# Three attention layers in one kernel: new due dates for the work between the attention steps, and rope computed in place

## The chip, the cores and the metric

One core of a Trainium2 chip runs the whole program. The core's engines work side by side, each with its own instruction queue: the tensor engine (PE in the profile; PEld is its weight load), the vector engine (DVE), the scalar engine (ACT), GpSimd (POOL) and the sync engine (SP), whose queue issues most of the transfers (DMA). The metric is the device time of one launch in microseconds. Lower is better.

## The reference, cut to what matters

The input `x` has 4 batches of 1024 tokens with 128 features. Four blocks follow one another, each of the form x + layernorm(block(layernorm(x))); all of it is float32. They are attention with 16 heads of 8 whose scores are clipped to [-10, 10]; a block with latent attention (heads of 64, half of which is rotated by position: rope) and a mixture of 8 experts; attention with 16 heads of 8 without the clip; and a low-rank feed-forward block with gelu.

```python
scores = jnp.clip(jnp.einsum('bhtd,bhsd->bhts', q, k) * SCALE, -10.0, 10.0) + mask   # first attention
q = jnp.concatenate([q_nope, _rope(q_rope)], axis=-1)                                # second
k = jnp.concatenate([kv, _rope(k_rope)], axis=-1)
x = x + _layernorm(_L0_attn_ref(_layernorm(x), ...))
x = x + _layernorm(_L0_ffn_ref(_layernorm(x), ...))
x = x + _layernorm(_L1_attn_ref(_layernorm(x), ...))
x = x + _layernorm(_L1_ffn_ref(_layernorm(x), ...))
```

## The kernel before

The program treats the work as three layers (classes `First`, `Second`, `Third`; the last feed-forward block is the tail of `Third`). A layer and a batch make a *stage*, twelve in all; a stage has four head groups `g` of four heads, and a stage and a head group make a *unit*: 48 units, numbered `n`, layer by layer and batch by batch. So units 0 to 15 are layer 1, 16 to 31 layer 2, and 32 to 47 layer 3.

**The main loop** (from line 1349) counts steps `at`, 20 to a unit. In each of ten iterations of a unit it issues the score products of one tile of keys (`scores`, the matmuls `ps_k<-strips`), the exponential on ACT with clip on DVE and causal cut on POOL (`weigh`, tile `pt`), and the products with the values of an earlier tile (`next_products`, the matmuls `av<-pt`). The argument of `next_products` says how many tiles may stay behind. Layers 2 and 3 subtract each row's maximum before the exponential. The maxima of a unit are made about one unit ahead, by `max_step` (matmuls `ps_q`, reductions on DVE into `mx`), at steps set by the queue `maxima`: 22 or 19 steps ahead of their unit. `negate` then sends the negated maxima by DMA into the unit's strips.

**Strips** are the tiles from which score products read queries and keys; there are three, unit `n` uses `n % 3`. `prepare(g, n)` of a layer fills them by DMA: from `packed` tiles in layers 1 and 3, from `rp` (rotated queries) and `lat` in layer 2, where the keys lie in a tile `kT` made by the preparation of the stage's first group. `roped` (line 661) does the rotation: ACT copies the product to `rb`, two DMAs write it with even and odd rows exchanged into `swapped`, DVE multiplies `rb` by the cosines into a new tile, and POOL multiplies `swapped` by the sines and adds it.

**All other work** is cut into pieces by Python generators (class `Task`). A piece says what it uses: LIGHT (vector, scalar, GpSimd or DMA work), SPARE or RING (a PSUM bank). There are intakes (`take_in`: normalise, transpose, project for a stage), preparations of units, tails of stages (`tail`: output projection, `add_normed`, experts), and `quarters` (the feed-forward of the last batch). After each iteration `other_work(at)` asks `pick` for pieces, up to four LIGHT ones and one of each other kind, and `pick` takes the task with the least slack: its due step, less the present step, less 1.35 for each piece that it has left. Nothing with a slack of 50 or more is taken, and unless it is late by 5, nothing while ACT or DVE are estimated to be behind PE. Due steps are 44 (layer 2), 28 (layer 3) or 8 (layer 1) ahead of the unit for a preparation, which can begin 48, 40 or 33 ahead; an intake is due 48, 40 or 33 ahead of its stage; a tail 5 steps before the end of the next stage.

**Forced work.** What is not done when it is needed is issued at once, in whole: `need_prep` before a unit and before its first maximum, `need_input`, `need_tail`, and `need_free(k)`, which runs a stage's tail until the result buffer that it reads (`att_free`) may be written again. It is called before the first result of a stage: with the stage before where either is of layer 2, otherwise with the stage before that, since the results lie in tiles of the tag `y` in `pool2` (`pool1` holds one of each tag, `pool2` two): a stage of layer 1 or 3 takes one, a stage of layer 2 both, one for each half of its tokens. A tail of layer 3 sets `att_free` when `add_normed` (line 427) has read the result in its first normalisation: statistics of 8 tiles on DVE (`stats`), the power -1/2 on POOL (`inv_root`), 8 scalings on ACT into `ynorm` (`scaled`), then two additions on POOL. In layers 1 and 2 it is set behind the first transposes.

PSUM's banks are given out in rotation: from layer 2 on a ring of 7 serves scores, maxima and most of the other work.

Of the kernel before, what the change touches and what calls it, by code (L numbers as in the profile page):

```python
# [138 lines left out]
def sandwich(ctx: ExitStack, tc: tile.TileContext, a: dict, out: bass.AP):  # L139
# [69 lines left out]
    w3_n = stage[:, 2048 : 2048 + 3 * D]  # L209
# [5 lines left out]
    later(out=w3_n, in_=a["L1_attn_w_qkv"])  # L215
# [66 lines left out]
    w3 = ctile([P, 3, D], "w3")  # L282
# [23 lines left out]
    def prepare_weights():  # L306
# [74 lines left out]
        nc.gpsimd.tensor_copy(w3.rearrange("p s e -> p (s e)"), w3_n)  # L381

# [87 lines left out]
    def project(packed, w, xT, copy):  # L470

        yield RING, 1
        t = pool2.tile([P, T], F32, tag=f"packed{len(packed)}", name="packed")
        packed.append(t)
        by_half(copy, t, product(w, xT, "ps_p"))
# [76 lines left out]
    class First:  # L552
# [43 lines left out]
        def take_in(self):  # L596
            self.xT = new_xT("xT1")
            self.unit = {}
            if self.b == 0:
                xn = pool1.tile([P, NT, D], F32, tag="xn", name="xn")  # L600
                self.packed = [pool2.tile([P, T], F32, tag=f"packed{s}", name="packed") for s in range(2)]
# [37 lines left out]
        def result(self, g, h):  # L639
            if g == 0 and h == 0:  # L640
                self.att = pool2.tile([P, NT, D], F32, tag="y", name="att1")
            return self.att[:, 4 * h : 4 * h + 4, 32 * g : 32 * g + 32]
# [18 lines left out]
    def roped(dst, w, xT):  # L661
# [6 lines left out]
        nc.vector.tensor_tensor(dst[0:n], rb[0:n], cos[0:n], ALU.mult)  # L668
        for c in range(2):
            yield LIGHT, 2 * (1 - c)  # L670
            cols = slice(512 * c, 512 * c + 512)
            nc.gpsimd.tensor_tensor(swapped[0:n, cols], swapped[0:n, cols], sin[0:n, cols], ALU.mult)  # L672
            nc.gpsimd.tensor_tensor(dst[0:n, cols], dst[0:n, cols], swapped[0:n, cols], ALU.add)

    class Second:
# [41 lines left out]
        def prepare(self, g, n):  # L717
            if g == 0:
# [3 lines left out]
                self.kT = pool2.tile([P, T], F32, tag="packed0", name="kT2")  # L722
# [3 lines left out]
                rp = pool2.tile([P, T], F32, tag="packed1", name="rpk")  # L726
                yield from roped(rp, wkr.rearrange("p j r -> p (j r)"), self.xT)
                yield LIGHT, 2
                for j in range(2):
                    nc.sync.dma_start(out=self.kT[64 * j + 32 : 64 * j + 64], in_=rp[32 * j : 32 * j + 32])  # L730
            if g % 2 == 0:
# [4 lines left out]
                by_half(nc.scalar.copy, lat, product(w, self.xT, "ps_l"))  # L736
            yield RING, 1
            rp = pool2.tile([P, T], F32, tag="packed1", name="rp")
            yield from roped(rp, w2r[:, 4 * g : 4 * g + 4].rearrange("p h r -> p (h r)"), self.xT)
            yield LIGHT, 2  # L740
            while step_now[0] < strips_free(n):
                yield LIGHT, 1
            t = self.unit[g] = strips[n % 3]
            nc.sync.dma_start(
                out=t[R:P:64].rearrange("o s (q c) -> o (s q) c", q=NT),
                in_=no_max[0:2].unsqueeze(1).to_broadcast([2, 2 * NT, P]),
            )
            for j in range(4):
                pp, at, h = j // 2, 64 * (j % 2), 4 * (g % 2) + j
                nc.sync.dma_start(out=t[at : at + R, pp, :], in_=self.lat[R * h : R * h + R, :])  # L750
                nc.sync.dma_start(out=t[at + 32 : at + 64, pp, :], in_=rp[32 * j : 32 * j + 32, :])
# [197 lines left out]
    class Third:  # L949
# [8 lines left out]
        def take_in(self):  # L958
            self.unit = {}
            self.xT = new_xT("xT3")  # L960
# [7 lines left out]
        def prepare(self, g, n):  # L968
            yield LIGHT
            if n < 2 * B * NG + 3:  # L970
                clear(strips[n % 3])
# [23 lines left out]
        def result(self, g, h):  # L995
            if g == 0 and h == 0:
                self.y = pool2.tile([P, NT, D], F32, tag="y", name="y3")
# [47 lines left out]
        def quarter(self, num, k):  # L1045
# [11 lines left out]
            if k == 1:  # L1057
                work, xb = tile("rb"), pool2.tile([P, T], F32, tag="packed0", name="xb")
# [70 lines left out]
    def ahead(u):  # L1129

        return (48, 44) if u.width == R else (40, 28) if u.has_max else (33, 8)
# [3 lines left out]
    units = [(layer[b], g) for layer in layers for b in range(B) for g in range(NG)]  # L1135
    stages = [u for layer in layers for u in layer]
    inputs = [Task(u.take_in(), u.pieces[0]) for u in stages]
    prep = [Task(u.prepare(g, n), (9, 4, 5, 4)[g] if u.width == R else 1) for n, (u, g) in enumerate(units)]
    tails = [None] * len(stages)
# [3 lines left out]

    def need_tail(k):

        while tails[k] is None or not tails[k].done:
            behind.popleft()[1].finish()

    def need_free(k):

        while not stages[k].att_free:
            behind[0][1].look(step_now[0])
            behind[0][1].piece(step_now[0])
            if behind[0][1].done:
                behind.popleft()

    def need_prep(n):
        for i in range(n + 1):
            if not prep[i].done:
                need_input(i // NG)  # L1160
                prep[i].finish()

    def need_input(k):
        for i in range(k + 1):
# [4 lines left out]

    def max_tiles(n):  # L1170

        mx, beside = {}, units[n][0].width != R
        for h in range(2):
            tiles = max_parts_of(h)
            if h and not beside:
                tiles = [tiles[i] for i in (0, 4, 1, 5, 2, 6, 3)]
            for i, parts in enumerate(tiles):
                for pp in (1, 0) if beside else (0, 1):
                    yield n, h, parts, pp, mx, i == len(tiles) - 1 and pp == 1 - beside

    def max_step(n, h, parts, pp, mx, last):
# [4 lines left out]
        ps = rtile("ps_q")  # L1186
        for qt, c, at, w in parts:
            for jj in range(2):
                q, k = u.rows(g, pp, jj)
                nc.tensor.matmul(  # L1190
# [239 lines left out]
```

## Time and profile before

| | |
|---|---|
| Runs | 2199.86, 2203.24, 2202.6 us: median 2202.6 |
| Profiled execution | 2196.13 us, of which the profile's span is 2194.4 |
| PE busy | 2062.8 us (94%), mean granted clock 0.974 |
| DVE, ACT, POOL busy | 1457.2 (66%), 1251.0 (57%), 589.5 (27%) us |
| Data moved by DMA | 42.93 MB in 32245 packets |
| Units 16, 32 and 47 begin | about 512.8, 1445.4 and 2109.4 us |

Busy time of an engine is time in which one of its instructions runs. The granted clock is the share of full speed that PE was allowed. A step is 1/20 of a unit, so that step 300 is the middle of unit 15, step 320 the start of layer 2, and step 640 that of layer 3.

### The profile page before, as it was taken

The page shows a single profiled execution, that of the slowest core. Times are in us where ns is not written, and L with a number is a line of the kernel's source. Part 1 is how long each engine was busy: PE and PEld are TensorE (multiplying, and loading weights), DVE is VectorE, ACT ScalarE, POOL GpSimd, SP SyncE. Part 2 cuts the span into 40 slices and gives each one's busy share as a digit, 9 for nine tenths or more (in the row PEclk, how much of TensorE's full clock was granted, in tenths as well). Part 3 has the DMA queues.
Part 4 walks back from the last instruction along what each step waited for, and adds up shares of the span by engine and source line. Part 5 has one row for each costly group of instructions (what it writes and reads, how often), then busy time and mean ns, then how long its engine had stood idle before and what let it go on. Part 6 is the DMA issues. An engine that isn't in the chain of part 4 may idle for free.

```text
span 2194.4 us, 40088 instructions
## 1 busy us (share of the span) xinstructions
PE 2062.8 (94%) x14480; PEld 939.4 (43%) x14480; DVE 1457.2 (66%) x4201; ACT 1251.0 (57%) x2360; POOL 589.5 (27%) x840
## 2 busy tenths in 40 slices
PE   7999999789999999999999999899999999999994
PEld 3334333334444544454444444344444444444432
DVE  4677776477666675567556675368778678777755
ACT  4777778524554554355534544255556766766775
POOL 3343333223232211222122311121113233323332
PEclk9999999989999999999999999899999999999996
DMA  2310000011111100111011100000000000000000
GB/s 59 69 17 11 12 11 11 21 38 25 28 42 26 25 16 22 35 29 26 6 30 35 29 13 1 11 7 7 6 7 7 12 7 16 8 11 17 7 1 20
DMA packets 32245, 42.93 MB, mean 20 GB/s; under 512 B 11552, under 2 KB 23840, under 8 KB 32048
## 3 DMA queue, kind: packets, MB, share of 16 engines
q1 hardware_dynamic: 31440, 40.04, 8.3%
q8 instruction: 115, 1.88, 0.3%
q14 instruction: 82, 0.67, 0.1%
q10 hardware_dynamic: 608, 0.33, 0.1%
HBM read 5.74 MB, written 2.10 MB: 4 GB/s over the span
## 4 chain that ended last, share of the span: by engine, by line
PE 82%; DVE 7%; ACT 5%; POOL 3%; issue 2%; DMA 1%; SPq 0%; ACTq 0%; POOLq 0%; DVEq 0%
PE ps_k L113 29%; PE ps_q L113 17%; PE av L113 17%; PE pgu L113 3%; ACT pt L113 2%; PE ps_a L113 2%; PE py L113 2%; DVE ps_q L113 2%; PE pa L113 2%; PE ps_p L113 1%; PE ps_o L113 1%; PE ps_t L113 1%; DVE mx L113 1%; DVE pt L113 1%; PE ps_l L113 1%
## 5 line engine op out<-in xcount | busy, mean ns | idle before, releaser
L113 ACT ACTIVATE pt<-ps_k 128x512 f32<-128x512 f32 (+2 forms) x1600 | 916.7, 631 | 621.4 <-PE ps_k L113 449.5
L1279 POOL TENSOR_SCALAR_AFFINE_SELECT pt<-pt 128x256 f32<-128x256 f32 (+1 forms) x576 | 302.8, 535 | 1209.4 <-ACT pt L113 887.4
L113 DVE CUSTOM_DVE_ANT_0 ps_q<-ps_q,cmask 128x512 f32<-128x512 f32 (+3 forms) x1024 | 488.4, 512 | 208.1 <-PE ps_q L113 187.6
L113 PE MATMUL ps_k<-strips 32*128 32x512 f32 (+3 forms) x3072 | 541.1, 527 | 9.8 <-DVE mx L113 4.9
L113 DVE TENSOR_REDUCE mx<-ps_q 128x1 f32<-128x512 f32 x512 | 328.3, 684 | 169.9 <-PE ps_q L113 168.5
L113 PE MATMUL ps_q<-strips 32*128 32x512 f32 (+3 forms) x1536 | 393.1, 530 | 14.1 <-DMA strips<-no_max 10.6
L113 PE MATMUL ps_q<-kT,strips 64*128 64x512 f32 (+3 forms) x1536 | 312.8, 491 | 25.1 <-DMA strips<-rp 24.2
L113 PE MATMUL av<-pt,vals 128*32 128x512 f32 (+3 forms) x3072 | 321.0, 500 | 15.7 <-POOL pt L1279 9.1
L113 PEld LDWEIGHTS ps_k<-strips 32*128 32x128 f32 x3072 | 220.2, 185 | 253.6 <-issue 76.3
L113 PE MATMUL ps_k<-strips,kT 64*128 64x512 f32 (+3 forms) x1536 | 323.3, 508 | 2.6 <-issue 2.6
L113 DVE TENSOR_SCALAR pt<-pt 128x1024 f32<-128x1024 f32 (+1 forms) x320 | 224.6, 717 | 115.7 <-ACT pt L113 114.1
L113 PEld LDWEIGHTS ps_q<-kT,strips 64*128 64x128 f32 x1536 | 150.0, 189 | 143.7 <-issue 100.5
L113 PEld LDWEIGHTS ps_k<-strips,kT 64*128 64x128 f32 x1536 | 133.9, 187 | 146.9 <-issue 66.2
L113 PEld LDWEIGHTS ps_q<-strips 32*128 32x128 f32 x1536 | 160.5, 184 | 64.8 <-ACT pt L113 26.2
L113 PEld LDWEIGHTS av<-pt,vals 128*32 128x32 f32 x3072 | 72.1, 109 | 218.6 <-issue 121.5
L113 PE MATMUL av<-pt,v2l 128*32 128x512 f32 (+3 forms) x1536 | 159.6, 503 | 0.0
L113 DVE DVE_READ_ACCUMULATOR2_ANT mx<- 128x1 f32 x1024 | 144.5, 141 | 0.0
L401 POOL TENSOR_TENSOR rs<-rs,minus_half 128x8 f32<-128x8 f32 (+1 forms) x38 | 63.6, 1674 | 242.4 <-DVE rs L113 239.6
L113 PEld LDWEIGHTS av<-pt,v2l 128*32 128x32 f32 x1536 | 33.7, 109 | 101.1 <-issue 72.7
L113 ACT COPY num<-av 128x512 f32<-128x512 f32 (+1 forms) x98 | 56.7, 581 | 19.8 <-PE av L113 19.7
L672 POOL TENSOR_TENSOR swapped<-swapped,sin 128x512 f32<-128x512 f32 (+1 forms) x40 | 50.8, 1271 | 63.1 <-DMA swapped<-rb 63.1
L113 PEld LDWEIGHTS ps_a<-ident,num 128*128 128x128 f32 x384 | 40.7, 141 | 61.7 <-issue 42.2
(278 smaller groups left out, 1646.0 us busy)
## 6 DMA issues: line engine op xcount, KB each, us to landing
swapped<-rb SPq DMA_DIRECT2D x32, 256.0 KB
strips<-rp SPq DMA_DIRECT2D x64, 128.0 KB
strips<-packed SPq DMA_DIRECT2D x248, 32.0 KB
strips<-lat SPq DMA_DIRECT2D x64, 64.0 KB
strips<-nT SPq DMA_DIRECT2D x256, 1.0 KB
strips<-nT SPq DMA_DIRECT2D x128, 2.0 KB
x<-in_L_attn_x_dram SPq DMA_DIRECT2D x3, 512.0 KB
out_dram<-x SPq DMA_DIRECT2D x3, 512.0 KB
```

Source lines behind the costliest of these rows:

```text
L113: return call(*args, **kw)
L401: nc.gpsimd.tensor_tensor(rs[:, t], rs[:, t], minus_half[:, t], ALU.pow)
L672: nc.gpsimd.tensor_tensor(swapped[0:n, cols], swapped[0:n, cols], sin[0:n, cols], ALU.mult)
L1279: nc.gpsimd.affine_select(out=corner, in_=corner, compare_op=ALU.is_ge, fill=0.0, base=0, pattern=[[0, 2], [0, n], [1, P]], channel_multip ...
```

## The change

The order of units stays. What changes:

- Due steps. A tail's due step (`due_tail`) is the old one or, where that is earlier, 28 steps ahead of the intake that needs it, or 30 ahead of the program's end for layer 3. An intake is due 34 (layer 1) or 48 steps ahead. It may begin only when all preparations of the previous stage of the same kind are done (`may_input`). Preparations of layer 1 begin 34 and are due 20 ahead; those of layer 3 are due 30 ahead. Tails are sorted by due step (`sort_behind`).
- Maxima. `lead` sets their start: 22 steps ahead of a unit in layer 2 but 20 for its first unit (16), 19 in layer 3, and for unit 32, the first of layer 3, two pairs of heads at a time (`together`) from 20 ahead.
- Other work. In layer 2 it is done twice in an iteration, with up to three LIGHT pieces each.
- Rope. The cosine product is written over `rb`, in two halves, each right ahead of the POOL operations of its half, two steps behind the copy; the sending of the rotated rows is a function that `roped` is given.
- Buffers. `kT` has a tag of its own in `pool2`; `packed` and the results of layers 1 and 3 move to `pool1`, the results under a tag `yb` (layer 2 keeps `y`). `need_free` is called with the previous stage of the same kind (`like`: layer 2, or layers 1 and 3 together).
- Weights of layer 3. They are no longer staged and copied by POOL at the start, but loaded into layer 1's weight tile when stage 8 is taken in.
- The last unit's products follow one iteration behind instead of two.

```diff
-    w3 = ctile([P, 3, D], "w3")
+    w3 = w1
...
-        t = pool2.tile([P, T], F32, tag=f"packed{len(packed)}", name="packed")
+        t = pool1.tile([P, T], F32, tag=f"packed{len(packed)}", name="packed")
...
-                self.att = pool2.tile([P, NT, D], F32, tag="y", name="att1")
+                self.att = pool1.tile([P, NT, D], F32, tag="yb", name="att1")
...
-                self.y = pool2.tile([P, NT, D], F32, tag="y", name="y3")
+                self.y = pool1.tile([P, NT, D], F32, tag="yb", name="y3")
...
-    def roped(dst, w, xT):
+    def roped(w, xT, send):
...
-        nc.vector.tensor_tensor(dst[0:n], rb[0:n], cos[0:n], ALU.mult)
         for c in range(2):
             yield LIGHT, 2 * (1 - c)
             cols = slice(512 * c, 512 * c + 512)
+            nc.vector.tensor_tensor(rb[0:n, cols], rb[0:n, cols], cos[0:n, cols], ALU.mult)
             nc.gpsimd.tensor_tensor(swapped[0:n, cols], swapped[0:n, cols], sin[0:n, cols], ALU.mult)
-            nc.gpsimd.tensor_tensor(dst[0:n, cols], dst[0:n, cols], swapped[0:n, cols], ALU.add)
+            nc.gpsimd.tensor_tensor(rb[0:n, cols], rb[0:n, cols], swapped[0:n, cols], ALU.add)
+        yield LIGHT, 2
+        yield from send(rb)
...
-                self.kT = pool2.tile([P, T], F32, tag="packed0", name="kT2")
+                self.kT = pool2.tile([P, T], F32, tag="kT", name="kT2")
...
-        return (48, 44) if u.width == R else (40, 28) if u.has_max else (33, 8)
+        return (48, 44) if u.width == R else (40, 30) if u.has_max else (34, 20)
...
+    def like(k):
+        same = [m for m in in_order if (stages[m].width == R) == (stages[k].width == R)]
+        return same[: same.index(k)]
+
+    def due_input(k):
+        return UNIT * starts[k] - (48 if stages[k].has_max else 34)
+
+    def due_tail(k):
+        return min([UNIT * (ends[k] + NG) - 5] + [due_input(k + B) - 28 if k < 2 * B else UNIT * len(units) - 30])
...
+    def may_input(k, at):
+        return (
+            at >= UNIT * (starts[k] - NG)
+            and (k < B or tails[k - B] and tails[k - B].done)
+            and all(t.done for m in like(k)[-1:] for t in preps(m))
+        )
+
+    def beside(n):
+        return units[n][0].width != R and units[n - 1][0].width != R
+
+    def together(n):
+        return n < len(units) and units[n][0].width != R and units[n - 1][0].width == R
...
-            if g == 0 and h == 0 and k > 0:
-                if u.width == R or stages[k - 1].width == R:
-                    need_free(k - 1)
-                elif k > 1:
-                    need_free(k - 2)
+            if g == 0 and h == 0:
+                for m in like(k)[-1:]:
+                    need_free(m)
...
+    def lead(n):
+        return 19 if beside(n) else 22 if units[n - 1][0].width == R and not together(n) else 20
...
+                wide = not u.has_max or n == len(units) - 1 or u.width != R and units[n + 1][0].width == R
+                often = u.width == R or u.has_max and wide and n < len(units) - 1
+                pts = []
+                for pps in ((0, 1),) if wide else ((0,), (1,)):
+                    pts += [weigh(n, h, parts, ps) for ps in scores(n, h, parts, pps)]
+                    if not u.has_max:
+                        next_products(1)
+                    for pp in pps:
                         at += 1
                         if maxima and maxima[0][0] <= at:
                             max_step(*maxima.popleft()[1])
-                        if pp == 0 and u.width != R:
+                        if pp == 0 and (u.has_max and (u.width != R or together(n + 1))):
                             next_products(0)
-                    if u.width == R:
-                        next_products(0)
-                other_work(at)
+                        if pp == 0 and often:
+                            other_work(at, 3)
+                if u.has_max:
+                    next_products(0)
+                other_work(at, 3 if often else 4)
```

## The prediction

> **What bounds the kernel.** I read the page first, then the waits, the timeline of the tensor engine (PE), windows around each hole in it, and the chain.
>
> ```profile
> span 2194.4 us, 40088 instructions
> PE 2062.8 (94%) x14480; PEld 939.4 (43%) x14480; DVE 1457.2 (66%) x4201; ACT 1251.0 (57%) x2360; POOL 589.5 (27%) x840
> PE   7999999789999999999999999899999999999994
> PEclk9999999989999999999999999899999999999996
> ```
>
> PE works 94% of the span. Its 131 us of idle time lie at the start, at the end and in slices 8 and 26, where the layers change and the clock drops too. The total of PE's work stays (the same 7614 matrix instructions stand in both programs), so a change of order is worth what it does to holes.
>
> The waits of PE name the releasers (idle us, times, longest):
>
> ```profile
> PE ps_q L113 <- DMA strips<-rp: 24.2, 3, 18.7
> PE ps_q L113 <- DMA strips<-no_max: 10.6, 1, 10.6
> ```
>
> The timeline shows where they stand (start, duration, and in brackets the idle time before):
>
> ```profile
> 445.99 3.18 PE L113 MATMUL ps_q<-kT,strips 64*128 64x512 f32 x4 [18.69 <-DMA strips<-rp]
> ...
> 883.44 2.40 PE L113 MATMUL ps_q<-kT,strips 64*128 64x512 f32 x4 [2.74 <-DMA strips<-rp]
> ...
> 1384.25 2.67 PE L113 MATMUL ps_q<-strips 32*128 32x512 f32 x4 [10.65 <-DMA strips<-no_max]
> 1466.32 3.84 PE L113 MATMUL ps_o<-w2o,attT 128*128 128x128 f32 x16 [2.78 <-ACT attT L113]
> ```
>
> All of these holes are the planner's: PE asks for strips, or for tail 7's transposes, in the step in which they are prepared. Behind each hole PE runs slowly (columns of the windows: PE, PEld, DVE, ACT, POOL busy, then the granted clock):
>
> ```profile
> 445.99:451.90 5.91, 5.91 (x20) 1.68 (x20) 2.36 (x6) 1.09 (x2) 0.35 (x1) 0.50 0.41 84
> 883.44:888.80 5.36, 5.32 (x14) 1.41 (x15) 1.56 (x5) 0.00 (x0) 0.00 (x0) 0.68 0.46 93
> 1127.50:1134.50 7.00, 7.00 (x15) 1.96 (x16) 1.55 (x5) 0.00 (x0) 0.00 (x0) 0.51 0.34 71
> 1384.25:1394.00 9.75, 9.75 (x30) 3.32 (x31) 2.81 (x8) 1.08 (x2) 0.42 (x1) 0.50 0.20 31
> 456.00:513.00 57.00, 50.68 (x308) 19.16 (x310) 48.84 (x137) 22.80 (x30) 17.31 (x20) 0.97 0.12 34
> ```
>
> So a hole costs itself and (1 - clock) of the window behind it: 18.69 + 3.0, 2.74 + 1.7, 10.65 + 4.9.
>
> **Part by part.** Steps are counted as in the planner, 20 to a unit; the order of the changed program shows what stands in which step.
>
> *First strips of layer 2 (unit 16).* Before, all ten pieces of its preparation are forced in step 298. Afterwards unit 15 is prepared at 284, so these pieces run from 284 to 298, and the first maximum comes at 300. The chain of waits shows what remains, from the second rope on (its last two lines belong to the end of the kernel, below):
>
> ```profile
> 425.34 2.31 DMA swapped<-rb
> ...
> 427.82 1.27 POOL swapped L672
> 429.15 2.12 POOL rpk L673
> ...
> 443.47 2.27 DMA strips<-rp
> ...
> 2141.04 1.65 POOL rs L401
> ...
> 2142.91 3.19 ACT ynorm L113 x8
> ```
>
> From the end of the product at 423.7 to the swap's landing 4.0, four POOL operations 4 x 1.27 = 5.1, issue and landing 0.6 + 2.3: 12 us after a product at step 294. PE has about 5.5 us of work until 300 (steps there take 2.1 us), so some 6.5 remain, with 2.5 of slow clock: 21.7 - 9 = 12.7 gained. Unit 15 is DVE's (48.84 of 57): two rope products of 1.225 and tail 2's statistics (3.2) leave it or spread, worth 3. Less contention below: **-15**. Bounds: -6 (the hole only moves) to -23 (it goes).
>
> *Later keys.* In steps 458 and 538 the last piece was forced beside the maximum that needs it; now it is done at 447 and 527. 2.74 + 1.7 and 2.76 + 3.4: **-10.6**.
>
> *First strips of layer 3.* Unit 32's strips move from step 620 to 600; the hole and its clock go: 10.65 + 4.9 = 15.5. Its maxima take both pairs of heads per step. Alone, a pair of 512 columns costs PE 1.06 us (4 instructions, 1406.29 to 1407.34); in layer 3, four-row-group neighbours start together (1628.88 and 1628.90) and share that time. Of 19.5 us of maxima half, 9.8, is saved, less 1 for four of seven banks taken at once. Tail 6's work leaves for units 28 to 30 at equal price. **-24** (-14 to -26).
>
> *No forced tail at step 649.* Tail 7's transposes are no longer forced, as layer 3 has no result buffer in common with layer 2: 2.78 + half of the 6.08 at clock 0.50 behind it, less 0.8 put back: **-5**.
>
> *The end.* Tail 10 is due at 930 instead of 955 and done by 944. Before, it ends in the chain: from its statistics at 2139.94 to 2146.10, 6.2 us. The quarters behind it wait partly for themselves: **-4**. The last unit's products now follow one step behind, not two, so PE waits for the exponential just issued: **+1.5** (0 to +4).
>
> *One result buffer in layers 1 and 3.* This is the price. Tails 8, 9 and 10 must pass their first normalisation before the next batch's first result: at steps 727, 807 and 887 the planner forces it in one burst. DVE: 8 statistics, 3.2 (four take 1659.08 to 1660.68); 0.2; POOL power 1.65; 0.2; ACT 3.19. ACT stands 5.2 and then works 3.2 before the next exponential: 8.4. Queued behind it are that exponential and the row copy, for which PE's products wait; behind DVE's wait for POOL, the maxima. PE has some 2 us queued, and the power operation of 1.65 and the ACT time are spared later (1.5 over the four steps after). 8.4 - 2 + 3.4 slow clock (as behind the 2.76 hole at 1124.7) - 1.5 = 8.3, three times: **+25**. Bounds 2 each (banks and pt buffers cover it) and 12.
>
> *Rope in place.* DVE multiplies in two halves of 0.69 (the 512-column product at 2176) for one of 1.225, +0.16 x 20, off the path. New: the product overwrites rb, so it waits for the swap to land; the maxima (or clips) are queued behind it. It stands two half steps, about 5 us, behind the PE product, and the landing takes 4.0. The old wait "DVE rp <- ACT rb" (20.9 us over 12) goes. Also rb stays taken until its sends land; the next rope's copy comes 13 us later. **+3** in all (-2 to +60, see the rivals). POOL's add took 2.12 instead of 1.27 beside a DVE product at 428.86; the halves now start with POOL's multiplication, up to 0.85 x 40 on POOL, which is 27% busy.
>
> The Trainium skill (SBUF — State Buffer, two separate sides) says that a DVE operation with two SBUF inputs and a reading GpSimd operation exclude each other for the whole instruction. It speaks against this placement; by it the remaining hole at step 300 would be 1.4 us longer (two halves of 0.69).
>
> The Trainium skill (TensorE: Matmul & The Clock Gate, why this matters for your kernels) lets idle gaps under about 3 us pass without throttling; the trace shows 0.68 behind 2.74. By the page the later keys would be worth 5.5 (the two holes alone).
>
> *No price:* layer 1's intakes wait for the previous batch's last strips (same pieces, ended 24 steps ahead of their use); w3 is loaded at step 560, 40 steps ahead; other work twice a step moves the same pieces, and layer 2's units stay PE's (idle at most 2.8 a unit). If that cover failed by 0.2 us a step, 150 steps would cost 30. Due dates of the other tails come out as before.
>
> **Sum.** -15 - 10.6 - 24 - 5 - 4 + 1.5 + 25 + 3 = -29.1. The profiled execution took 2196.1 (span 2194.4), 6.5 below the median of the runs: span 2165.3, profiled 2167.0, median 2173.5.
>
> **Rivals.** (a) *Bursts hidden*, 2 each (6 for 25): -48: 2154.5. For it: ACT is idle a third of layer 3; against it: nothing but queued work covers a chain of five operations. (b) *Holes move*: unit 16 gains only 6 (+9), the pairs 5 less, bursts 11 each (+8): -7: 2195.5. For it: a deadline that is met late by 5 us of DMA is a hole again. (c) *Slower*: DVE waits for the swap in each of 20 ropes and PE with it, about 3 us (the landing from its issue, 2.3 + 0.5): 60 in place of 3, +28: 2230.5. It makes the kernel slower from 1.6 us a rope on (32 / 20). Against it: the landing comes before the product's turn; for it: DVE is the engine that holds layer 1's last units. That the change does nothing is excluded by the moved steps.
>
> **Chances.** Forecast 0.47, (a) 0.21, (b) 0.17, (c) 0.15. Range 2146 to 2204: (a) less 8, and (b) with 8 more of worst bounds; (c) and the tip of (a) are left out. Under 0.2% (4.4 us) is about no change to this kernel's measurement. Of (b), 0.10 lies below 2198, 0.05 within, 0.02 above: faster 0.78, same 0.05, slower 0.17.
>
> **To be seen.** Right: no wait of ps_q for strips over 8 us; clock 1.0 at the start of layer 3; three holes of PE around 6 us at about a quarter, a half and three quarters of layer 3 (steps 727, 807, 887 of 640 to 960), with ACT waiting for nb; no ynorm in the last chain. Wrong: holes of PE behind DVE's rb in layer 2, or no holes at steps 727, 807, 887.

## The result

The changed kernel takes 2209.87 us (median of 6 runs, 2207.65 to 2212.94), the kernel before 2201.98 in the same runs: a ratio of 1.0037, 95% interval 1.0024 to 1.0050. It is slower by some 8 us, where 2173.5 was forecast. The profiled execution took 2211.2 us, its span is 2209.5. The two profiled executions lie 15 us apart, not 8: that of the kernel before was 5.9 us below its median, this one 1.3 above.

Head of the page of the changed kernel:

```profile
span 2209.5 us, 40126 instructions
PE 2078.2 (94%) x14480; PEld 932.4 (42%) x14480; DVE 1474.3 (67%) x4221; ACT 1246.2 (56%) x2360; POOL 593.8 (27%) x839
PE   7989998979999999999999999999999999999995
PEclk9999999989999999999999999999999999999996
```

Slice 26 is full now and the clock there is back. PE's idle time is 131.3 us (2209.5 - 2078.2), as before. But the same instructions keep PE busy 15.4 us longer (2062.8 before): holes have gone, and work has become slower. The waits of PE (idle us, times, longest):

```profile
PE av L113 <- POOL pt L1329: 19.6, 25, 1.8
PE ps_q L113 <- DVE mx L113: 16.9, 13, 4.2
PE ps_k L113 <- DVE mx L113: 8.3, 10, 4.3
PE ps_ct L113 <- DVE comb L113: 6.5, 3, 4.5
PE ps_q L113 <- DMA strips<-rb: 6.3, 1, 6.3
```

The 24.2 and 10.6 us behind strips are down to one hole of 6.3, so the moves that the prediction counted did take place. The other four rows are mostly new. The same waits of the kernel before:

```profile
PE av L113 <- POOL pt L1279: 9.1, 14, 1.6
PE ps_q L113 <- DVE mx L113: 0.9, 4, 0.3
```

The timeline of PE in the changed kernel, at the hole ahead of unit 16 and at one behind the maxima, and the windows around the first (columns as before):

```profile
449.70 3.15 PE L113 MATMUL ps_q<-kT,strips 64*128 64x512 f32 x4 [6.25 <-DMA strips<-rb]
...
1656.05 2.66 PE L113 MATMUL ps_q<-strips 32*128 32x512 f32 x4 [3.86 <-DVE mx L113]
```

```profile
443.50:449.75 6.25, 0.05 (x1) 0.08 (x1) 3.49 (x5) 0.00 (x0) 6.17 (x6) 0.71 0.19 41
449.75:457.00 7.25, 7.25 (x12) 2.41 (x16) 3.30 (x10) 0.38 (x1) 1.12 (x3) 0.54 0.33 68
```

The forecast had 6.5 us for the hole ahead of unit 16. POOL works through nearly all of it (6.17 of 6.25 us): the rope is what PE waits for. The second line of the timeline is the burst at step 727. Those at 807 and 887 have holes of 4.2 us, where three of around 6 were to be seen.

**Where the time went.** A unit is measured here from its first score product to that of the next one, in the timelines. Lengths in us; the last column is the forecast for the row, from the prediction's terms.

| units | before | changed | difference | forecast |
|---|---|---|---|---|
| 0 to 11 | 323.6 | 331.5 | +7.9 | 0 |
| 12 to 15 | 170.5 | 164.8 | -5.7 | -15 |
| 16 to 30 | 859.7 | 884.9 | +25.2 | -7.6 |
| 31, 32 | 123.1 | 84.4 | -38.7 | -29 |
| 33 to 46 | 613.8 | 645.3 | +31.5 | +25 |
| 47 to the end | 85.0 | 80.1 | -4.9 | -2.5 |

Work moves between the rows: some 8 us of tail 6's matrix work stand in units 28 to 30 instead of 31 to 33. It moves inside a row too: units 21 and 25 got 21 and 19 us longer, but 22 and 23, and 26 and 27, got 17 and 19 us shorter. So units 16 to 19 grew by 6 us, 20 to 27 by only 4, and 28 to 30 by 15. Most of the first row is the clock and no sure effect of the change: units 0, 3, 6 and 10 hold one stretch of 3.4 us each at clock 0.50. alternate_results (below) has the changed order of units 0 to 11, but one such stretch, and took 326.0; kernels ordered as before took 323.6 to 328.8. Overhead, in the expectations below, is a unit's length less what its matrix instructions would take by their sizes alone.

### The profile page after: what moved, and what is told of

The parts are those of the page before. It is cut to its first block, busy times and chain, and to the rows that moved or that the text cites. A ratio compares the mean times of both kernels' runs of the same rounds, so it can differ in the third digit from the quotient of the medians.

```text
span 2209.5 us, 40126 instructions
## 1 busy us (share of the span) xinstructions
PE 2078.2 (94%) x14480; PEld 932.4 (42%) x14480; DVE 1474.3 (67%) x4221; ACT 1246.2 (56%) x2360; POOL 593.8 (27%) x839
## 4 chain that ended last, share of the span: by engine, by line
PE 79%; DVE 8%; ACT 6%; POOL 3%; issue 2%; DMA 1%; SPq 0%; ACTq 0%; DVEq 0%; POOLq 0%
PE ps_k L113 28%; PE av L113 17%; PE ps_q L113 15%; PE pgu L113 3%; ACT pt L113 3%; PE ps_a L113 2%; DVE ps_q L113 2%; PE py L113 2%; PE pa L113 2%; PE ps_p L113 1%; DVE mx L113 1%; PE ps_t L113 1%; PE ps_o L113 1%; PE ps_v L113 1%; DVE pt L113 1%
## 5 line engine op out<-in xcount | busy, mean ns | idle before, releaser
L113 PE MATMUL ps_q<-strips 32*128 32x512 f32 (+3 forms) x1536 | 382.4, 531 | 13.6 <-DVE mx L113 12.6
L113 PE MATMUL av<-pt,vals 128*32 128x512 f32 (+3 forms) x3072 | 346.5, 511 | 24.8 <-POOL pt L1329 19.6
L113 PE MATMUL ps_k<-strips,kT 64*128 64x512 f32 (+3 forms) x1536 | 331.7, 515 | 4.6 <-DVE mx L113 2.5
L113 PEld LDWEIGHTS ps_q<-kT,strips 64*128 64x128 f32 x1536 | 147.8, 188 | 132.0 <-issue 83.9
L113 PEld LDWEIGHTS av<-pt,vals 128*32 128x32 f32 x3072 | 81.8, 109 | 240.5 <-issue 121.0
L113 PEld LDWEIGHTS ps_q<-strips 32*128 32x128 f32 x1536 | 156.0, 186 | 54.8 <-ACT pt L113 21.5
L113 PE MATMUL ps_a<-ident,num 128*128 128x128 f32 x384 | 63.7, 288 | 0.0
L669 POOL TENSOR_TENSOR rb<-rb,swapped 128x512 f32<-128x512 f32 (+1 forms) x40 | 57.1, 1427 | 15.3 <-POOL swapped L668 7.9
```

The source lines that it names most:

```text
L113: return call(*args, **kw)
L669: nc.gpsimd.tensor_tensor(rb[0:n, cols], rb[0:n, cols], swapped[0:n, cols], ALU.add)
```

## The experiments

Each was timed beside the kernel before on the same chip; medians in us.

### The result buffers

My first theory was the prediction's: the single result buffer forces bursts in layer 3. **two_results** puts both results back into the tag of before:

```diff
-                self.y = pool1.tile([P, NT, D], F32, tag="yb", name="y3")
+                self.y = pool2.tile([P, NT, D], F32, tag="y", name="y3")
...
-                for m in like(k)[-1:]:
-                    need_free(m)
+                if k > 0 and (u.width == R or stages[k - 1].width == R):
+                    need_free(k - 1)
+                elif k > 1:
+                    need_free(k - 2)
```

(and the same for `att1`).

> The changed kernel, but the results of layers 1 and 3 lie again in the two-buffer tag y, and the result buffer is asked for as before the change. Theory A (one result buffer forces the first normalisation of tails 8, 9 and 10 in one burst; units 36, 40 and 44 got 8.3, 8.4 and 9.6 us longer): they fall back to 39 to 41 us, some 25 us go, about 5 come back with the transposes of tail 7 forced at the start of layer 3: 2190 us (2185 to 2196). Rival (the bursts only show where work stands that has to be done anyway, so the steps after give it back): 2204 or more, with units 37 to 39 longer by what 36 saves.

Measured: 2212.81. Units 36, 40 and 44 fell by 8.5, 7.8 and 8.8 us, 25 in all, as expected, and still nothing was won. Unit 12, where the single buffer had forced a part of tail 2, fell by 5.6 as well. Against that, tail 7's transposes came back with 14 us in units 32 to 35 instead of 5, units 42 and 46 grew by 5 each, and the end by 5.4. The timelines of unit 42 show how, first PE, then POOL:

```profile
1906.45 1.45 PE L113 MATMUL av<-pt,vals 128*32 128x256 f32 x8 [4.22 <-POOL pt L1331]
```

```profile
1900.29 1.64 POOL L397 TENSOR_TENSOR rs<-rs,minus_half 128x8 f32<-128x8 f32 x1 [2.23 <-DVE rs L113]
1902.01 0.62 POOL L1032 TENSOR_SCALAR sq<-sq 128x512 f32<-128x512 f32 x1
1902.71 1.27 POOL L1033 TENSOR_TENSOR sq<-sq,xb 128x512 f32<-128x512 f32 x1
1904.06 0.62 POOL L1032 TENSOR_SCALAR sq<-sq 128x512 f32<-128x512 f32 x1
1904.76 1.26 POOL L1033 TENSOR_TENSOR sq<-sq,xb 128x512 f32<-128x512 f32 x1
1905.98 1.18 POOL L1331 TENSOR_SCALAR_AFFINE_SELECT pt<-pt 128x256 f32<-128x256 f32 x3
```

The causal cut of `pt`, for which PE's products wait, is queued behind a power and four operations of a tail: 5.7 us from the power's start. POOL is 27% busy over the span and holds PE up all the same.

**alternate_results** avoids both costs: batches 0 and 2 of layers 1 and 3 use `yb`, 1 and 3 use `y`, and no tail is forced at step 649 or in the bursts.

```diff
-                self.y = pool1.tile([P, NT, D], F32, tag="yb", name="y3")
+                pool, tag = ((pool1, "yb"), (pool2, "y"))[self.b % 2]
+                self.y = pool.tile([P, NT, D], F32, tag=tag, name="y3")
...
-                for m in like(k)[-1:]:
+                for m in [k - 1] if u.width == R else [k - 2] if k in (2, 3, 9, 10, 11) else []:
```

> The changed kernel with the results of layers 1 and 3 in yb and y in turn, and nothing else (rope in place as the change has it). If rope in place costs what it cost beside two_results (15.7 us), this stands at 2184.0 + 15.7 = 2200 (2196 to 2204), and the single result buffer costs 10 us net, not the 26 by which units 36, 40 and 44 grew. Rival (the two costs are not additive, and the buffers are worth their 26 us): 2184 to 2192.

Measured: 2198.61. The single buffer costs 11.3 us net. In the profiles it costs 23.5 in its three units and 5.6 in unit 12, and gives back 15.4 in units 42, 46 and 47.

### Rope in place

**two_results_rope_apart** gives the rope a buffer, with one product right behind the copy:

```diff
+        rp = pool1.tile([P, T], F32, tag="rp", name="rp")
+        nc.vector.tensor_tensor(rp[0:n], rb[0:n], cos[0:n], ALU.mult)
         for c in range(2):
...
-            nc.vector.tensor_tensor(rb[0:n, cols], rb[0:n, cols], cos[0:n, cols], ALU.mult)
...
-        yield from send(rb)
+        yield from send(rp)
```

> As two_results, with the rope's cosine product in a buffer of its own again, in one piece right behind the copy, and the rotated rows sent from there. The trace of the changed kernel shows no wait of DVE for the swap in the list of waits, so the theory is no difference from two_results within 3 us. Rival (c) of the prediction, the product over the copy makes DVE wait for the swap: faster than two_results by 10 us or more.

Measured: 2197.06, 15.7 us faster than two_results. I was wrong to read the list of DVE's waits as an acquittal: DVE's own wait for the swap is 0.7 us in all in the changed kernel, and 3.0 in two_results. Most of the loss sits elsewhere. (alternate_results beside alternate_rope_apart, below, gives the price once more: 14.6.) In the changed kernel's timeline of the first rope, POOL, then DVE:

```profile
424.98 2.96 POOL L668 TENSOR_TENSOR swapped<-swapped,sin 64x512 f32<-64x512 f32 x1 [4.87 <-DMA swapped<-rb]
428.01 1.59 POOL L669 TENSOR_TENSOR rb<-rb,swapped 64x512 f32<-64x512 f32 x1
429.57 1.72 POOL L668 TENSOR_TENSOR swapped<-swapped,sin 64x512 f32<-64x512 f32 x1
431.36 1.61 POOL L669 TENSOR_TENSOR rb<-rb,swapped 64x512 f32<-64x512 f32 x1
```

```profile
424.91 1.28 DVE L113 TENSOR_TENSOR rb<-rb,cos 64x512 f32<-64x512 f32 x2 [0.27 <-DMA swapped<-rb]
426.12 5.71 DVE L113 TENSOR_SCALAR pt<-pt 128x1024 f32<-128x1024 f32 x4
```

Four POOL operations take 7.9 us where 4 x 1.27 = 5.1 were reckoned, and a clip on DVE 1.43 in the mean (5.71 / 4) where one alone takes 0.69 (at 423.94). **rope_apart_late** keeps the separate buffer and puts the product, in halves, back beside POOL's operations:

```diff
-        nc.vector.tensor_tensor(rp[0:n], rb[0:n], cos[0:n], ALU.mult)
...
+            nc.vector.tensor_tensor(rp[0:n, cols], rb[0:n, cols], cos[0:n, cols], ALU.mult)
```

> As two_results_rope_apart, with a buffer of its own for the rotated rows, but the cosine product in two halves, each right ahead of POOL's operations of its half, as the change has it. Two readings of the 15.7 us between two_results (2212.8) and two_results_rope_apart (2197.1). Theory P (place: the product of two SBUF tiles meets POOL's operations; in the changed kernel 28 of POOL's 80 rope operations took over 1.4 us, before 2): as two_results, 2207 to 2216. Rival W (the wait: the product over the copy has to wait until the swap has landed, and its buffer until the rows are sent): as two_results_rope_apart, 2193 to 2201.

Measured: 2201.76, between the two. The place costs 4.7 us; writing over the copy, with the wait for the swap and a buffer held until the sends land, costs 11.0. The split is rough, as the five runs of two_results lie between 2206.9 and 2216.5; by the lengths of units 14 to 26 the place costs 6.8 and the overwriting 5.7. Unit 14 shows the second: ACT's copy for the next rope waits until the rows of the last one have left `rb`, and PE waits behind that copy. First ACT and PE in two_results, then the same copy in two_results_rope_apart:

```profile
432.95 1.07 ACT L113 COPY rb<-pa 128x512 f32<-128x512 f32 x2 [5.13 <-DMA kT<-rb]
434.08 2.66 PE L113 MATMUL ps_o<-w,att1T 128*128 128x128 f32 x16 [3.25 <-ACT rb L113]
```

```profile
427.43 1.07 ACT L113 COPY rb<-pa 128x512 f32<-128x512 f32 x2 [1.02 <-issue]
```

The hole ahead of unit 16 is not where the loss lies: it is 3.5 us in two_results and 5.1 with the rope apart.

**before_rope_in_place** does nothing but the change's rope to the kernel before:

> The kernel before the change, with nothing but the rope computed in place, as the change has it. Theory (rope in place costs in itself, by its waits and by meeting POOL's reads): 8 to 18 us slower than before, 2209 to 2219. Rival (it costs only where the new due dates put a rope beside the work that needs it): within 4 us of before.

Measured: 2234.9, 33 us slower, twice what the theory allowed. The waits of PE in it:

```profile
PE ps_q L113 <- DMA strips<-rb: 45.0, 3, 22.4
```

Before, they were 24.2, 3, 18.7. Holes that were there got longer (18.7 to 22.4 at the maxima of unit 16, 2.7 to 10.3 and 2.8 to 12.3 at those of units 24 and 28). DVE waits 24.2 us for the swap here, in four places. The new `roped` also cuts a stage's first preparation into one piece more, so that at step 458 POOL's four operations are forced, not the sends alone: POOL's timeline has them inside the hole, which ends at 899.2, from 891.1 to 896.7. So this run prices the longer preparation together with the overwriting, and the price is a matter of what waits behind the rope.

### Other work twice, and the intakes

Units 21, 25 and 29 had grown by 21, 19 and 18 us, and theory B blamed the second call of other work; its rival the later intakes. **other_once** sets `often = False`:

> The changed kernel, with other work once in an iteration of layer 2, up to four light pieces, as before the change. Theory B (twice an iteration packs the tails' and intakes' pieces into fewer steps, where DVE is full and PE waits; overhead of units 21, 25 and 29 over the work of PE rose by 10.5, 8.9 and 5.7 us): layer 2 gets some 20 us shorter, 2190 us (2184 to 2197). Rival C (the packing comes from the intakes, which may begin only when the last strips of the stage before are made): layer 2 stays within 5 us, 2205 to 2213.

Measured: 2241.67, 32 us slower than the changed kernel. Units 21, 25 and 29 did fall by 21, 21 and 18, but 22 and 26 rose by 19 and 18, so that most of this is work that moves. In all, units 16 to 30 grew by 5.6, units 31 and 32 by 9, and units 33 to 46 by 16 (unit 35 alone by 21: its intake and the strips of unit 36 are late, and PE waits 4.7 for them). The hole at step 458 came back at its worst:

```profile
901.60 3.33 PE L113 MATMUL ps_q<-kT,strips 64*128 64x512 f32 x4 [12.35 <-DMA strips<-rb]
```

**intakes_early** undoes the intakes' rule:

```diff
-        return UNIT * starts[k] - (48 if stages[k].has_max else 34)
+        return UNIT * starts[k] - ahead(stages[k])[0]
...
-            and all(t.done for m in like(k)[-1:] for t in preps(m))
```

> The changed kernel, with the intakes' rule of before the change: no waiting for the preparations of the previous like stage, due 33, 48 or 40 ahead. Theory C (the later intakes pack DVE's work in layer 1 and in layer 2): layer 1 up to unit 13 gets some 10 us shorter and layer 2 some 15: 2185 to 2197. If theory B alone holds, layer 1 gets 5 to 10 us shorter and layer 2 stays: 2200 to 2206. Rival (the loss of layer 1 comes from the result buffer): no difference, 2207 to 2213.

Measured: 2225.18. All three theories miss: layer 2 wins 8.3 us (units 16 to 30), layer 3 loses 19 (units 33 to 46), 11 of them in unit 35, where PE waits 4.7 us for the strips of unit 36, as in other_once. Perhaps an early intake of layer 3 waits there for the preparations that still read the single `packed` buffers; no run takes that apart. (The intakes of layer 1 were due 34 ahead in this run, not 33.)

Next I put the good together. **alternate_rope_apart** has alternate buffers and the rope apart (in `yb`, which is free in layer 2), **alternate_rope_intakes12** also the old rule for the intakes of layers 1 and 2, and **alternate_rope_intakes12_once** drops the second call again.

> The changed kernel with two edits: the results of layers 1 and 3 lie in turn in yb and in y, so that neither a burst nor the transposes of tail 7 are forced, and the rope's product lies apart, right behind the copy, in yb. Theory: of the changed kernel's 2209.9 the bursts go (25), the forced pieces of unit 12 (5.6) and the rope's price (16); two_results lost some 10 us in units 42 and 46 and 6 at the end for its gain, which may return here: 2178 us (2163 to 2190). Rival (the gain of two_results was lost to other places for good, whatever buffers are used): 2194 or more.

> As alternate_rope_apart, with the intakes of layers 1 and 2 by the rule of before the change; layer 3 keeps the new rule. From intakes_early: layer 2 gives 8 us; layer 1 gives the 8 us that units 0 to 11 lost, now that no result buffer forces tails into the same steps: 10 to 16 us faster than alternate_rope_apart. Rival (the intakes of layer 1 meet the tails wherever they stand): within 9 us of it or slower.

> As alternate_rope_intakes12, with other work once in an iteration of layer 2. Theory B (twice an iteration packs units 21, 25 and 29): 6 to 15 us faster than alternate_rope_intakes12. Rival (twice lets tails 4 to 7 end in time; once leaves their pieces to be forced later, as in other_once, where units 22 and 26 took 84 us): 10 to 30 us slower.

Measured: 2184.02, 2179.13 and 2210.32. The costs of buffers and rope add up (11.3 + 15.7 = 27.0, measured 25.9). The intakes of layers 1 and 2 are worth 4.9, half of the least that was expected. One call costs 31 us, so the rival of theory B stands: with the new due steps the second call is what ends this work in time. With one call PE waits for strips again, where it waited 5.7 in one place:

```profile
PE ps_q L113 <- DMA strips<-rp: 20.7, 3, 11.4
```

Does it help by more pieces or by spreading them? **alternate_rope_intakes12_light2** allows two light pieces a call, four an iteration as before; **before_twice** adds the second call to the kernel before.

```diff
+                        if pp == 0 and u.width == R:
+                            other_work(at, 3)
...
-                other_work(at)
+                other_work(at, 3 if u.width == R else 4)
```

> As alternate_rope_intakes12 (2179.1), with two light pieces at each of the two calls of other work in layer 2 instead of three, so four an iteration as before the change. Theory (it is the number of light pieces that makes the deadlines): holes come back, 2195 to 2212, as with one call. Rival (it is their spreading over the iteration): 2172 to 2184, with units 21, 25 and 29 shorter.

> The kernel before the change, with nothing but other work twice an iteration in layer 2, up to three light pieces each. Theory (twice is what lets the last piece of a preparation end ahead of the maximum that needs it): no hole behind DMA strips at steps 458, 538 and 620, 5 to 20 us faster: 2181 to 2196. Rival B (packing the pieces costs, the due dates remove the holes): the holes stay and layer 2 gets longer: 2203 to 2220.

Measured: 2181.54 and 2181.67. Two light pieces a call do as well as three, so it is not their number. It may be the spreading, as the rival has it, but units 21, 25 and 29 did not get shorter (75.7, 75.7 and 78.1 us for 74.6, 76.2 and 76.6), and two calls also allow two pieces of each bank kind in an iteration instead of one: no run separates these. By itself the second call gives 20 us: the holes at 458, 538 and 620 are gone from the waits, the one at unit 16 stays. The gain lies in units 31 and 32 (123.1 to 102.0, some 8 of it moved work). Units 16 to 30 stay at 859.3: two holes are gone, and the moved work has come in.

```profile
PE ps_q L113 <- DMA strips<-rp: 18.7, 1, 18.7
```

### The due steps alone

What, then, did the due steps give? **before_strips16** changes three numbers of the kernel before:

```diff
-        return (48, 44) if u.width == R else (40, 28) if u.has_max else (33, 8)
+        return (48, 44) if u.width == R else (40, 28) if u.has_max else (34, 20)
...
-        (UNIT * n + i - (22 if units[n][0].width == R else 19), m)
+        (UNIT * n + i - (22 if units[n][0].width == R and n > B * NG else 20 if n == B * NG else 19), m)
```

**before_pairs** has the change's `max_tiles` and `max_step`, with unit 32's maxima in pairs (and, as in the change, unit 31's products issued half an iteration earlier). **before_twice_strips16_pairs** is both and the second call, **before_twice_strips16** the same without pairs, and **changed_no_pairs** and **alternate_rope_intakes12_no_pairs** take the pairs out of kernels that had them.

> The kernel before the change, with preparations of layer 1 from 34 ahead and due 20 ahead, and the maxima of unit 16 from step 300. As maxima are handed out one a step, those of all of layer 2 then follow two steps later, at 460 and 540 instead of 458 and 538, and the last pieces of units 24 and 28 are no longer forced. The prediction's terms: 15 for unit 16 and 10.6 for the later keys: 2176 (2172 to 2181). Rival (without the second call the chains behind those pieces still end too late, and the holes only move): 2186 to 2202.

> The kernel before the change, with nothing but both pairs of heads of unit 32's maxima in one step. The strips of unit 32 are still made at step 620, so the hole of 10.65 stays; of the prediction's 24 us only the pairs are left: 8.8 (half of 19.5, less 1): 2193 (2190 to 2196). Rival (four banks at once and DVE's reductions eat it): 2199 to 2206.

> The kernel before the change, with three things of the change: other work twice an iteration in layer 2, the preparations of layer 1 earlier with the maxima of unit 16 from step 300, and unit 32's maxima in pairs from step 620 (its strips are then made at 600). Theory (the other due steps, the single result buffer and the rope in place all cost, and nothing that they cost is needed by these three): before_twice's 2181.7 less 14 at units 14 and 15 and 17 at units 31 and 32: 2151 (2144 to 2162). Rival (the gains overlap: what twice gives is what the due steps give): 2165 to 2182.

> The kernel before the change with two things of the change: other work twice an iteration in layer 2, and the preparations of layer 1 earlier with the maxima of unit 16 from step 300. Theory (what is left of before_twice's hole goes, and layer 3 stays as before): 2201 less 20, less 21 at unit 14: 2158 (2150 to 2166). Rival (the two remove the same holes): 2166 to 2176.

> The changed kernel with unit 32's maxima one pair of heads a step, from 19 ahead, as before the change; all else as changed. If the pairs shift the rest of layer 3 to its cost as in before_pairs, units 33 to 47 get some 15 to 20 us shorter, units 31 and 32 some 10 to 16 longer: 2200 to 2208. Rival (the prediction's term holds: the pairs save half of the maxima and nothing else moves): 2214 to 2224, with units 33 to 47 as in the changed kernel.

> As alternate_rope_intakes12 (2179.1), with unit 32's maxima one pair of heads a step from 19 ahead, as before the change. Theory (the pairs move layer 3's other work to worse steps, in before_pairs by 23 us): units 33 to 47 get some 20 us shorter, units 31 and 32 some 8 to 15 longer: 2164 to 2174. Rival (in the changed kernel it is the intakes, which wait for the single packed buffers): units 33 to 47 stay, 2184 to 2196.

Measured, with lengths of units:

| kernel | median | 12 to 15 | 16 to 30 | 31, 32 | 33 to 46 |
|---|---|---|---|---|---|
| before_strips16 | 2169.91 | 147.8 | 851.8 | 117.2 | 617.0 |
| before_pairs | 2221.72 | 172.6 | 875.8 | 104.5 | 636.2 |
| before_twice_strips16_pairs | 2179.96 | 148.7 | 872.5 | 91.2 | 634.1 |
| before_twice_strips16 | 2171.27 | 149.2 | 871.2 | 102.1 | 614.4 |
| changed_no_pairs | 2218.19 | 165.2 | 883.8 | 93.3 | 649.5 |
| alternate_rope_intakes12 | 2179.13 | 155.1 | 874.1 | 84.3 | 634.9 |
| alternate_rope_intakes12_no_pairs | 2190.72 | 156.9 | 872.9 | 97.4 | 630.4 |

before_strips16 is the fastest of all: ratio to before 0.9864, interval 0.9837 to 0.9891. From its page, PE, and from its waits, the only one for strips:

```profile
PE 2056.4 (95%) x14480; PEld 933.2 (43%) x14480; DVE 1461.6 (68%) x4201; ACT 1248.6 (58%) x2360; POOL 590.0 (27%) x840
PE   7999999999999999999999998999999999999994
```

```profile
PE ps_q L113 <- DMA strips<-no_max: 7.7, 1, 7.7
```

The hole of 18.7 at unit 16 has gone altogether, with its slow clock, and so have those of the later keys; only unit 32's is left. The second call then adds nothing (2171.27): it closes that hole (102.1 for 117.2) and lengthens units 16 to 30 by 19.5, of which some 8 is moved work. The two remove the same holes, as the rival said.

The pairs behave in two ways. In the changed kernel, and with its costs undone, they are worth 8.3 and 11.6 us. Put into the kernel before, they cost 20, outside both expectations, and beside before_twice_strips16 they cost 8.7: units 33 to 46 take 22 and 20 us longer. In the traces most of the tails' power operations there stand two to four steps earlier; that this is the cause is not shown. The last experiment was to show that this is also what layer 3 loses in the changed kernel. That theory fell: without the pairs, units 33 to 46 stay at 630.4.

## Why the prediction was wrong

The step that failed first is "*No price:* ... other work twice a step moves the same pieces, and layer 2's units stay PE's": units 16 to 30 were to get 7.6 us shorter and got 25.2 longer. Next to it, rope in place was put at +3 and measured 15.7, and layer 3 takes 20 us more than before even without the bursts, a term that was not in the sum. The holes themselves were priced nearly rightly.

**Right.** *First strips of layer 2* (-15) and *later keys* (-10.6): -25.6, with before_strips16 at -31.3; units 12 to 15 gave 22.7 and 16 to 30 gave 7.9. The holes did cost themselves and their clock. That no hole stayed at unit 16 there, where 6.5 us were reckoned, was not foreseen. In the changed kernel the hole of 6.25 is as reckoned, but units 12 to 15 gave only 5.7 of the 15: the single buffer took 5.6 back in unit 12, and the rope 4.7 in unit 14. *First strips of layer 3* and *no forced tail*: -29 against -38.7 for units 31 and 32. *The end*: -2.5 against -4.9. The burst was sized well. ACT's timeline at step 727:

```profile
1655.49 3.18 ACT L113 ACTIVATE ynorm<-y,nb,rs 128x128 f32<-128x128 f32 x8 [4.38 <-DVE nb L113]
```

ACT stood 4.4 and then worked 3.2 us, where 5.2 and 3.2 were reckoned, and the three units grew by 26.3, where 25 were forecast. PE's holes were shorter than reckoned (3.9 and twice 4.2 for some 6), so the sum came out better than its parts.

**Rope in place, "+3 in all (-2 to +60)"**: 15.7 measured. Only DVE, the engine that carries the new wait, was priced. That `rb` stays taken until its sends land was named, with the next copy 13 us later; but at unit 14 the next copy did have to wait for them, 5.1 us in two_results and 3.1 in the changed kernel, and PE behind it. And POOL's operations and DVE's clips held each other up. Rival (c) had the direction; the size was 0.8 us a rope, for its 3 and below the 1.6 from which it was to decide, and other terms did the rest. Its mechanism, DVE waiting for the swap, is 0.7 us in the changed kernel and counts only in before_rope_in_place (24.2). The rule of the Trainium skill (SBUF — State Buffer, two separate sides) was in the prediction, with 1.4 us at one hole. The runs put the place at 4.7 (6.8 by the units). They agree with the page that the two engines hold each other up, and its condition is wider than I used it: it names DVE operations in a two-port mode too, which would fit the clips at 1.43, though no run here shows in which mode they ran.

**One result buffer, "+25"**: right in the units where it falls, 11.3 net. Unit 12's 5.6 was not in the sum. The bursts also cleared POOL's power operations out of later steps; without them units 42 and 46 pay 5 each and the end 5.4. A gross price was put into a sum of net ones.

**"No price: other work twice a step", "layer 1's intakes wait"**: this is the largest miss. Beside before_strips16 the second call lengthens units 16 to 30 by 11 us over the moved work. Beside the kernel before it lengthened them by some 2, counted in the same way, so the price depends on which pieces then meet; which these are was not separated. And the holes' closing, which I had credited to due steps, is at the same time the second call's own work: 20 us before, 31 in the changed kernel, nothing beside before_strips16. Of the 33 us that the sum missed in units 16 to 30, some 8 are moved work, 11 this, 5 the rope beyond its +3, 3.5 the intakes, and 5 have no name. "Layer 2's units stay PE's (idle at most 2.8 a unit)" came from idle time, and the loss became longer busy time for the most part. In units 16 to 30 the same 1440 score products of the profile cover 9.2 us more of PE's busy time than before (310.7 for 301.5). The timelines of PE and DVE in unit 22 show one such case, at matmuls of the maxima, and below each the same instructions undisturbed:

```profile
910.05 2.27 PE L113 MATMUL ps_q<-kT,strips 64*128 64x512 f32 x4
912.25 1.07 PE L113 MATMUL av<-pt,v2l 128*32 128x512 f32 x8
...
803.74 1.02 PE L113 MATMUL ps_q<-kT,strips 64*128 64x512 f32 x4
```

```profile
906.79 1.23 DVE L113 SCALAR_TENSOR_TENSOR nb<-mv,rs 128x8 f32<-128x8 f32 x1
...
1645.21 0.16 DVE L113 SCALAR_TENSOR_TENSOR nb<-mv,rs 128x8 f32<-128x8 f32 x1
```

Four such instructions take 1.02 us when the two row groups run side by side (at 803.74). Here the second group started 1.14 us after the first, and PE counts as busy for all but 0.12 us of it. The DVE operation, on 8 columns, took 1.23 us beside a POOL operation (0.16 at 1645.21). How much of the 9.2 us is of this kind was not added up.

**Missing from the sum**: layer 3 without the bursts still takes 20 us more than before (alternate_results, 634.2 against 613.8). It isn't the pairs (630.4 without them, with the costs undone) and not the buffers of results. In the kernels that kept layer 3's order of pieces, or nearly, units 33 to 46 took 614 to 617, in all others 630 to 664, and `av` waits 9 to 10 us for POOL in the former and 18 to 24 in the latter. That POOL's queue is the cause in all of them is argued, not shown; which of the new due steps and single `packed` buffers sets that order was not separated.

By the profiles' rows, the sum missed 44 us (by the medians 36): 33 in units 16 to 30, 9 in 12 to 15, 8 in 0 to 11 (most of it the clock), 6.5 in 33 to 46, less 12 in the last and in units 31 and 32. That units 33 to 46 come so near is luck: the bursts' 25 was gross, and the 20 were not in the sum.

## What to carry to other kernels

Take one term of such a change at a time: three numbers of this one gave 31 us, and the rest, which looked like free cleaning up, took 40 back. Under a planner that fills gaps, price a moved piece by what is queued behind it on every engine, above all on a lightly loaded one whose few operations others wait for. And look at the length of busy stretches as well as at holes: a PE that waits for the second of two row groups is busy in the profile.

## What the runs showed of the hardware

- After an idle gap of PE of 3.86 us, ending at 1656.05, the granted clock was 0.50 for the next 5 us. After one of 18.69 us (the kernel before) it was 0.50 for 5.9 us, after one of 10.65 for 9.75. From the windows of the changed kernel:

```profile
1656.05:1661.00 4.95, 4.95 (x12) 1.54 (x12) 1.83 (x3) 4.69 (x12) 2.53 (x2) 0.50 0.00 0
```

- POOL's rope operations, 1.27 us undisturbed, took up to 2.96 beside DVE's work, and DVE's halves of the product (0.68) up to 1.78.
- Units 0 and 3 took 62.2 us together in the kernel before, with the granted clock at 1.00 in both, and 66.0 in the changed one, with 3.4 us at 0.50 in each. Kernels with the order of before there took 62.2 to 65.8.
